# Expert weights and the first batch's denominators brought to their rows by transfers through HBM

## The chip, the cores and the metric

The kernel runs on one core of a Trainium2 chip. The metric is the device time of one execution in microseconds. A core has five engines that run at the same time: TensorE (PE, matrix products), VectorE (DVE), ScalarE (ACT), GpSimd (POOL) and SyncE (SP). In this kernel nearly all transfers between HBM and the on-chip memory (SBUF) are issued by SP, in the order of its own queue. Products of PE land in eight banks of a second memory, PSUM.

## What is computed

The reference is one transformer layer on `x` of 2 x 1024 tokens with 512 features, in float32. The layer adds two branches to its input, both computed from the normalised `xn`:

```
Q, K, V = heads(xn @ w.T + b)            # 16 heads of 32 features
Q, K = elu(Q) + 1, elu(K) + 1
out_attn = (Q @ (K^T V)) / (Q . sum(K) + 1e-8)  ->  @ wo.T + bo
scores = sigmoid(xn @ W_router)          # 8 experts
w = the two best of scores + bias, normalised; 0 elsewhere
gate = xn @ W_gate + shared low-rank + sum_e w_e * (xn @ A_e @ B_e)
up   = the same with its own matrices
out_ffn = (silu(gate) * up) @ W_down + low-rank terms
x + out_attn + out_ffn
```

Two values of this matter here. The **expert weights** `w` have one number for each token and expert; the kernel multiplies them into the low-rank factors `xn @ A_e`, which have 8 rows for each expert (rank 8), for gate and up. The **denominators** have one number for each token and head, and each divides the 32 features of its head.

## The kernel before

The 2048 tokens are two batches of 1024 (`NBATCH`), each in two groups `g` of 512 tokens (`TB`). Features lie on the 128 partitions in four chunks `c` of 128 (`NC`). The large products use seven block products in place of eight, so sums and differences of blocks are made on DVE and POOL. The order of the work on PE, DVE, ACT and POOL is the order of the program's text (`manual_schedule`, L67); SP's queue is ordered by the scheduler, by when data and buffers are ready.

The stages around the change, at 120 to 250 us of the profile:

- `query_unit(0)` (L957) makes the queries of batch 0. It calls hooks at named points (P2, P1, P6, P5, P7, P3, P4), after the products of the same number; a hook runs other work that is written into the order there. `route(n)` (L562) ranks the experts of group n and gives `ws[n]`, the tokens' expert weights, with tokens on the partitions.
- After it (L968 to L988): `shared_factors`; `load_weights(0)`, which loads the first gate and up weights; `spread_weights` (L590), which repeats each weight 8 times and for gate and up on POOL; `weights_across` (L600), which turns the spread weights by 4 transposes per group on PE and copies them by ACT to `wT[b]`, where rows are (gate or up, expert, rank) and columns are tokens; `low_rank_in` (L846), products with the factors `A`, times `wT` on DVE (L852), giving `xa`; `denominators(0)` (L856), 8 products and a reciprocal (L866), giving `den`, in which row `c * 32 + 8 * h + 4 * g` belongs to chunk c, head h of the chunk and group g; the last token sums of batch 1; `token_diffs` (L980) on POOL.
- `rest_weights` (L1006) loads and prepares the last 96 columns of gate and up.
- `query_unit(1)` (L1080) makes the queries of batch 1. Its hooks run `attend(0, g)` (L869): four products of a 0/1 matrix `spread` with `den` bring each denominator to the 32 rows of its head in PSUM, DVE multiplies the query tile by it (L878) and SP stores the tile (L881). `fold_rest(i)` (L1023) adds the shared low-rank term to the rest weights: 4 small products, 8 DVE additions (L1032).
- Then `low_rank_in(2)` and `(3)`, `denominators(1)`, `rest(0, ...)` (L1034), in which `fold(0, 0)` adds the low-rank term to the first gate weights (L938), and `attend(1, ...)`.

Tiles are taken from pools: a tile with a tag waits until the last use of the tile that had the buffer before. The pool for PSUM gives out eight banks.

Of the kernel before, what the change touches and what calls it, by code (L numbers as in the profile page):

```python
# [15 lines left out]
P = 128  # L16
# [21 lines left out]
def layer_kernel(  # L38
# [53 lines left out]
    NQ = UT // P  # L92
    NPQ = NC // 2
    WARM = 18

    TILES = [b * TPBATCH + g * TPB + t for b in range(NBATCH) for t in range(TPB) for g in range(2)]

# [16 lines left out]
    h_dram = [[dram.tile([2, P, 4, UT], F32, name=f"h_dram{b}_{j}") for j in range(NP)] for b in range(NBATCH)]  # L114
    r_dram = [dram.tile([2, REST, 2, UT], F32, name=f"r_dram{b}") for b in range(NBATCH)]
    q_dram = [[dram.tile([2, P, 4, UT], F32, name=f"q_dram{b}_{j}") for j in range(NPQ)] for b in range(NBATCH)]
    kvo_dram = [dram.tile([P, NC, D], F32, name=f"kvo_dram{b}") for b in range(NBATCH)]

    ffn_stack = ExitStack()
# [22 lines left out]
    def hold(v):  # L142

        nc.vector.memset(v, 0.0)
# [142 lines left out]
    def norm(n):  # L287

        k = n % 6
        xns[n] = (  # L290
            p1w.tile([P, D], F32, tag=f"xn{k}", name=f"xn{n}", bufs=1)
            if k < 4 else p2w.tile([P, D], F32, tag=f"qt{k - 2}1", name=f"xn{n}", bufs=1)
        )
# [261 lines left out]
    def shared_factors(i):  # L555
# [3 lines left out]
        )  # L559
        nc.scalar.mul(sat[:, i, :], pa[:, 0:P], SCALE)  # L560

    def route(n):  # L562

        sc = p2.tile([P, TPB, E], F32, tag="sc", name=f"sc{n}")
        nc.scalar.activation(sc, lg[n], AF.Sigmoid)
        bi = p2.tile([P, TPB, E], F32, tag="bi", name=f"bi{n}")
        nc.vector.tensor_add(bi, sc, eb_sb.unsqueeze(1).to_broadcast([P, TPB, E]))

        sh = [P, TPB, E, E]
        bj = bi.unsqueeze(2).to_broadcast(sh)  # L570
        be = bi.unsqueeze(3).to_broadcast(sh)
        gt = p2.tile(sh, F32, tag="gt", name=f"gt{n}")
        nc.vector.tensor_tensor(gt, bj, be, ALU.is_gt)
        eq = p2.tile(sh, F32, tag="eq", name=f"eq{n}")
        nc.vector.tensor_tensor(eq, bj, be, ALU.is_equal)
        nc.vector.tensor_mul(eq, eq, before.unsqueeze(1).to_broadcast(sh))
        nc.vector.tensor_add(gt, gt, eq)
        rank = p2.tile([P, TPB, E], F32, tag="rank", name=f"rank{n}")
        nc.vector.tensor_reduce(rank, gt, AX.X, ALU.add)
        ws = p2.tile([P, TPB, E], F32, name=f"ws{n}")  # L580
        nc.vector.scalar_tensor_tensor(ws, rank, TOP_K - 0.5, sc, ALU.is_lt, ALU.mult)
        sm = p2.tile([P, TPB], F32, tag="sm", name=f"sm{n}")
# [5 lines left out]
        return ws  # L588

    def spread_weights(n):  # L590

        wx = p2.tile([P, TPB, 2, ER], F32, tag="wx", name=f"wx{n}", bufs=2)
        for t in range(TPB):
            nc.gpsimd.tensor_copy(
                wx[:, t, :, :].rearrange("p i (e r) -> p i e r", r=RANK),
                ws[n][:, t, :].unsqueeze(1).unsqueeze(3).to_broadcast([P, 2, E, RANK]),
            )
        return wx

    def weights_across(n, wx):  # L600
        pw = bank(f"pw{n}")
        for t in range(TPB):
            nc.tensor.transpose(pw[:, ts(t, P)], wx[:, t, :, :].rearrange("p i r -> p (i r)"), ident)
        nc.scalar.copy(wT[n // 2][:, ts(n % 2, TB)], pw)

    tsum = []
    tsum_pair = []
# [69 lines left out]
    ws = {}  # L677

    def routed(n):
        ws[n] = route(n)  # L680

    hooks = {
        (1, "b"): [lambda: load_weights(wq_sb, wqT)],
# [11 lines left out]
        (7, "a"): [lambda: routed(0), lambda: fin[0].outputs((1,))],  # L695
        (7, "b"): [lambda: fin[0].outputs((2, 3))],
    }

    def load_weights(t, w):
        hold(t[:, 0, 0:1])  # L700
        nc.sync.dma_start(out=t, in_=by_chunk(w))
# [149 lines left out]
            nc.tensor.matmul(pa, agu_sb[:, c, :], xt(b, c, cols), start=(c == 0), stop=(c == NC - 1))  # L851
        nc.vector.tensor_mul(xa[b][:, cols], pa, wT[b][:, cols])  # L852

    dens = {}

    def denominators(b):  # L856

        pd = bank(f"pd{b}")
        for g in range(2):
            for c in range(NC):  # L860
                nc.tensor.matmul(
                    pd[c * 32 : (c + 1) * 32, :], ksd[b][:, g, c, :], qt[b, c, g], start=(g == 0), stop=(g == 1)
                )
        den = ffn.tile([P, TB], F32, tag="den", name=f"den{b}")
        nc.vector.tensor_scalar_add(den, pd, DIV_EPS)
        nc.vector.reciprocal(den, den)  # L866
        dens[b] = den

    def attend(b, g):  # L869

        pb = []
        for c in range(NC):
            rows = slice(c * 32, (c + 1) * 32)
            pb.append(bank(f"pb{b}_{g}_{c}"))
            nc.tensor.matmul(pb[c], spread[rows, g, :], dens[b][rows, :], start=True, stop=True)
        for c in range(NC):
            v = qt[b, c, g]
            nc.vector.tensor_mul(v, v, pb[c])  # L878

            j, i = c % NPQ, c // NPQ  # L880
            nc.sync.dma_start(  # L881
                out=q_dram[b][j][:, :, 2 * i + g, :].rearrange("s p n -> p s n"),
                in_=v.rearrange("p (s n) -> p s n", n=UT),
            )
# [5 lines left out]

    wsum = {}

    def load_weights(j):

        ws = []
        for i, w in enumerate((w_gate, w_up)):
            if j % 2 and i == 0:
                t = slot(8, [8, 2 * P], f"w{i}_{j}")
            elif j % 2:
                t = tsp.tile([P, 8, 2 * P], F32, tag="t3", name=f"w{i}_{j}")  # L900
            else:
                t = tsp.tile([P, 8, 2 * P], F32, tag=f"t{i}", name=f"w{i}_{j}")
            v = t.rearrange("p s (k m) -> p s k m", m=P)
            for half in range(2):
                f = (j + half * NP) * P
                nc.sync.dma_start(
                    out=v[:, 6 * half : 6 * half + 2, :, :].rearrange("p s k m -> p (s k) m"),
                    in_=by_chunk(w)[:, :, f : f + P],
                )
            ws.append(t)  # L910

        sb = ffn.tile([P, 2, 2, P], F32, tag="sb", name=f"sb{j}", bufs=2)
        for i, w in enumerate((b_gate, b_up)):
            for k in range(SG):
                nc.sync.dma_start(
                    out=sb[k * 32 : k * 32 + RANK, i, :, :],
                    in_=w[ER:LR, 0 : 2 * NP * P].rearrange("r (h n) -> r h n", h=2)[:, :, ts(j, P)],
                )
        wsum[j] = (ws, sb)
# [28 lines left out]
    def last_sums():  # L948
        add_keys(late)
        for args in late:  # L950
            accumulate(*args)
        for n in (1, 2):
            routed(n)
        fin.append(Finish(1, pg, ksum))
        fin[1].copies()

    query_unit(0, {  # L957
        "P2": [last_sums],
        "P6": [lambda: fin[1].chunk_sums(), lambda: fin[1].sums(), lambda: routed(3)],
        "P5": [lambda: fin[1].values()],  # L960
        "P7": [lambda: next(sums1), lambda: next(sums1)],
        "P3": [lambda: fin[1].outputs((0, 1, 2, 3))],
    })
    psum1.close()
# [4 lines left out]
        shared_factors(i)  # L969
    p1_stack.close()  # L970
    tsp = pool(ctx, "tsp", side="right")
    load_weights(0)
    wx = [spread_weights(n) for n in range(2)]
    for n in range(2):
        weights_across(n, wx[n])
    low_rank_in(0)
    low_rank_in(1)
    xdiff = []

    def token_diffs(b, tag):  # L980
# [53 lines left out]
    def rest(b, between=(None, None)):  # L1034
# [1063 lines left out]
```

## Time and profile before

| | us |
|---|---|
| median of 3 runs | 731.14 |
| lowest, highest | 730.44, 731.93 |
| profiled execution | 732.03 |
| its span | 730.2 |
| PE busy in the span | 719.9 (99%) |
| DVE busy | 579.99 |
| ACT, POOL busy | 199.80, 147.25 |
| PE clock granted | 0.996 |

The span is what the profile covers of the execution; 1.8 us lie around it. A row of a timeline gives start, duration, engine, line, operation, output and input tiles, shapes and a count; in brackets stands the idle time before it and what ended it. A float32 product of PE is two records. In the chain of work each piece is followed back to what released it. `SPq` rows are transfers being issued, not their data. Buffer numbers are left out of names: `pw` is `pw0` to `pw3`.

### The profile page before, as it was taken

How to read it: one execution, taken by the hardware profiler on the slowest of the kernel's cores; microseconds unless marked ns; L12 is line 12 of the kernel's file. 1: busy time of each engine (PE TensorE's matmuls, PEld its weight loads, DVE VectorE, ACT ScalarE, POOL GpSimd, SP SyncE). 2: the span in 40 equal slices, each digit the busy share in tenths (PEclk: the TensorE clock that was granted, in tenths of full speed). 3: DMA queues.
4: the chain of work that ended last, by engine and by line, in shares of the span. 5: the costliest groups of instructions: out<-in, count | busy, mean ns of one | idle time of the engine just before them, and what ended most of it. 6: DMA issues, size and time to landing. Idle time of an engine off the chain costs nothing.

```text
span 730.2 us, 9892 instructions
## 1 busy us (share of the span) xinstructions
PE 719.9 (99%) x3458; PEld 494.6 (68%) x3458; DVE 580.0 (79%) x1326; ACT 199.8 (27%) x440; POOL 147.3 (20%) x192
## 2 busy tenths in 40 slices
PE   8999999999999999999999999999999999999997
PEld 6666676454433556666666666666688899899896
DVE  6788766776777688878878878968888889998874
ACT  3534513454433323323333333333200000000000
POOL 4023011112000680410410410543520100000000
PEclk9999999999999999999999999999999999999999
DMA  5343000207314101211201201334653444523101
GB/s 168 98 130 116 1 0 37 61 1 188 120 29 126 37 5 57 88 33 58 87 29 58 87 29 59 111 121 144 202 180 117 125 146 134 166 95 110 58 17 43
DMA packets 59398, 63.37 MB, mean 87 GB/s; under 512 B 10066, under 2 KB 48594, under 8 KB 59092
## 3 DMA queue, kind: packets, MB, share of 16 engines
q1 hardware_dynamic: 58818, 62.72, 28.0%
q8 instruction: 27, 0.44, 0.3%
q14 instruction: 23, 0.19, 0.1%
q10 hardware_dynamic: 530, 0.02, 0.0%
HBM read 40.97 MB, written 21.76 MB: 86 GB/s over the span
## 4 chain that ended last, share of the span: by engine, by line
PE 84%; DVE 12%; ACT 1%; issue 1%; DMA 0%; DVEq 0%; ACTq 0%
PE ab L1179 16%; PE b L1239 8%; PE po L1875 7%; PE pg L398 5%; PE pqu L772 4%; PE pya L1747 4%; PE pxa L1747 3%; PE pyb L1747 3%; PE ph L1615 3%; PE x L1179 3%; PE pxb L1747 2%; PE pyc L1747 2%; PE b L1234 2%; PE pqv L772 2%; PE pxa L851 2%; PE pr L1073 2%
## 5 line engine op out<-in xcount | busy, mean ns | idle before, releaser
L1239 PE MATMUL b<-t,w 128*128 128x512 f32 x160 | 83.2, 601 | 0.8 <-DVE t L1261 0.8
L398 PE MATMUL pg<-kt,xn 128*128 128x512 f32 x128 | 58.7, 594 | 0.5 <-DVE kt L342 0.5
L1261 POOL TENSOR_TENSOR r<-r,r 128x512 f32<-128x512 f32 x20 | 30.1, 1524 | 84.6 <-DVE t L1261 83.0
L1179 PE MATMUL ab<-ti,wi 128*128 128x256 f32 x180 | 45.4, 379 | 0.0
L1179 PEld LDWEIGHTS ab<-ti,w 128*128 128x128 f32 x140 | 25.2, 189 | 29.5 <-DVE r L1207 8.3
L1261 DVE TENSOR_TENSOR r<-r,r 128x512 f32<-128x512 f32 x60 | 45.0, 791 | 0.0
L1179 PEld LDWEIGHTS ab<-ti,wi 128*128 128x128 f32 x180 | 34.2, 190 | 13.2 <-issue 5.0
L1179 PE MATMUL ab<-ti,w 128*128 128x256 f32 x140 | 41.2, 387 | 0.5 <-DVE r L1207 0.2
L398 PEld LDWEIGHTS pg<-kt,xn 128*128 128x128 f32 x128 | 23.1, 190 | 22.6 <-issue 20.6
L1212 ACT COPY r<-ab 128x256 f32<-128x256 f32 x50 | 18.6, 373 | 71.5 <-PE ab L1179 71.5
L1239 PEld LDWEIGHTS b<-t,w 128*128 128x128 f32 x160 | 29.2, 190 | 11.3 <-issue 5.9
L1207 DVE TENSOR_TENSOR r<-r,ab 128x256 f32<-128x256 f32 x50 | 21.0, 419 | 19.8 <-ACT r L1204 19.2
L1215 DVE TENSOR_TENSOR r<-r,ab 128x256 f32<-128x256 f32 x50 | 20.9, 418 | 16.2 <-ACT r L1212 15.8
L1189 ACT COPY r<-ab 128x256 f32<-128x256 f32 x50 | 18.6, 373 | 48.5 <-PE ab L1179 47.0
L1875 PE MATMUL po<-wd,f 128*128 128x256 f32 x140 | 30.9, 380 | 0.1
L407 POOL TENSOR_TENSOR ksum<-ksum,kt 128x512 f32<-128x512 f32 x12 | 15.8, 1320 | 71.7 <-DVE lg L444 42.3
L1200 ACT COPY r<-ab 128x256 f32<-128x256 f32 x50 | 18.6, 373 | 40.8 <-PE ab L1179 40.8
L1818 DVE TENSOR_TENSOR f<-f 128x256 f32<-128x256 f32 x84 | 29.4, 423 | 0.1
L1875 PEld LDWEIGHTS po<-wd,f 128*128 128x128 f32 x140 | 26.4, 190 | 4.4 <-issue 0.5
L1179 PE MATMUL ab<-xnT,w 128*128 128x256 f32 x100 | 29.4, 390 | 0.0
L1179 PE MATMUL ab<-xnT,wi 128*128 128x256 f32 x100 | 28.1, 379 | 0.0
L1179 PEld LDWEIGHTS ab<-xnT,w 128*128 128x128 f32 x100 | 18.1, 189 | 10.8 <-issue 4.3
(449 smaller groups left out, 1665.3 us busy)
## 6 DMA issues: line engine op xcount, KB each, us to landing
h_dram<-h SPq DMA_DIRECT2D x40, 256.0 KB
f<-h_dram SPq DMA_DIRECT2D x10, 512.0 KB
x_ring<-in_x_dram SPq DMA_DIRECT2D x16, 256.0 KB
q_dram<-qt SPq DMA_DIRECT2D x16, 256.0 KB
xr<-in_x_dram SPq DMA_DIRECT2D x16, 256.0 KB
out_dram<-xr SPq DMA_DIRECT2D x15, 256.0 KB
w<-in_w_gate_dram SPq DMA_DIRECT2D x10, 256.0 KB
w<-in_w_up_dram SPq DMA_DIRECT2D x10, 256.0 KB
```

Source lines behind the costliest of these rows:

```text
L398: nc.tensor.matmul(pg[m], xns[n][:, ts(m, P)], kt, start=(j == 0), stop=(j == TPBATCH - 1))
L772: nc.tensor.matmul(banks[c], wqs[p][:, k, ts(c, P)], tsum[b][p][:, k, :], start=(start and k == 0), stop=(k == 1), skip_group_check=True,)
L1179: nc.tensor.matmul(out, w, t, start=start, stop=True, skip_group_check=True)
L1189: nc.scalar.copy(self.r[0][:, H0], self.ua)
L1207: nc.vector.tensor_add(self.r[1][:, H1], self.r[1][:, H1], self.lo)
L1215: nc.vector.tensor_add(self.r[1][:, H0], self.r[1][:, H0], self.lo)
L1239: nc.tensor.matmul(pb[m], ws[m][:, A_OF[p], ts(k, P)], tsum[b][p][:, k, :], start=start, stop=True, skip_group_check=True)
L1261: eng.tensor_add(to[m], t[m], v[m])
L1615: nc.tensor.matmul(phs[u][g * ER : (g + 1) * ER, :], a, f[:, g, :], start=(ns[0] == 0 and n == 0), stop=(last and n == len(chunks) - 1), s ...
L1747: nc.tensor.matmul(o, lhsT, rhs, start=first, stop=True, skip_group_check=True)
L1818: op(t[:, at, :], t[:, x_, :], t[:, y, :])
L1875: nc.tensor.matmul(ps[p][:, q, :], lhsT, rhs, start=start, stop=stop, skip_group_check=True)
```

## The change

Expert weights: `route` writes the weights of both groups of a batch into one tile `wts[b]`. `weights_across(b)` transposes that tile once on PE (128 x 64), ACT copies it to `wx`, SP stores it to HBM (`w_dram`), and 16 transfers read it back, each copying one expert's 1024 weights to 8 rows of `wT[b]`. It is called in `query_unit(0)` at P5 (batch 0) and P7 (batch 1). `spread_weights` is gone.

Denominators of batch 0: `den` is stored to HBM (`d_dram`). `spread_den` reads four of its rows back, each to the 32 rows of a head, into one of three tiles `bc`; three such tiles are filled at once and the next after each multiplication. The multiplications come in four pairs, at P5, P7, P3 and P4 of `query_unit(1)`. Batch 1 keeps the products.

Around it: the low-rank products, `denominators(0)` and `token_diffs(0)` follow `rest_weights`, with `denominators(0)` between the two low-rank products; `load_weights(0)` moves to P4 of `query_unit(1)`, where small memsets on DVE hold its transfers back; `fold_rest(1)` moves from P4 to after `load_last`. Some tiles share buffers: `gt` takes a `tmp` buffer, `rank` that of `bi`, three `xn` tiles those of `bc`.

```
+    wts = [p2.tile([P, 2, TPB, E], F32, name=f"ws{b}") for b in range(NBATCH)]
...
-        gt = p2.tile(sh, F32, tag="gt", name=f"gt{n}")
+        gt = p2w.tile(sh, F32, tag="tmp", name=f"gt{n}", bufs=3)
...
-        rank = p2.tile([P, TPB, E], F32, tag="rank", name=f"rank{n}")
+        rank = bi
...
-        ws = p2.tile([P, TPB, E], F32, name=f"ws{n}")
+        ws = wts[n // 2][:, n % 2]
...
-    def spread_weights(n):
...
-    def weights_across(n, wx):
-        pw = bank(f"pw{n}")
-        for t in range(TPB):
-            nc.tensor.transpose(pw[:, ts(t, P)], wx[:, t, :, :].rearrange("p i r -> p (i r)"), ident)
-        nc.scalar.copy(wT[n // 2][:, ts(n % 2, TB)], pw)
+    def weights_across(b):
+        rows = 2 * TPB * E
+        pw = fin[1].bank(f"pw{b}")
+        nc.tensor.transpose(pw[0:rows, 0:P], wts[b].rearrange("p n t e -> p (n t e)"), ident)
+        wx = p2.tile([rows, P], F32, tag="wx", name=f"wx{b}")
+        nc.scalar.copy(wx, pw[0:rows, 0:P])
+        nc.sync.dma_start(out=w_dram[b].rearrange("e t p -> t e p"), in_=wx)
+        for i in range(2):
+            for e in range(E):
+                k = i * ER + e * RANK
+                nc.sync.dma_start(
+                    out=wT[b][k : k + RANK, :],
+                    in_=w_dram[b][e].rearrange("t p -> (t p)").partition_broadcast(RANK),
+                )
...
+    def spread_den():
+        i = len(bcs)
+        if i == 2 * NC:
+            return
+        g, c = divmod(i, NC)
+        t = p2w.tile([P, TB], F32, tag=f"bc{i % NBC}", name=f"bc{i}", bufs=1)
+        for h in range(HPC):
+            row = c * 32 + 8 * h + 4 * g
+            nc.sync.dma_start(out=t[h * DK : (h + 1) * DK, :], in_=d_dram[row, :].partition_broadcast(DK))
+        bcs[i] = t
...
         dens[b] = den
+        if b == 0:
+            nc.sync.dma_start(out=d_dram, in_=den)
+            for i in range(NBC):
+                spread_den()
...
-    def attend(b, g):
+    def attend(b, g=None):
+        if b:
...
+        else:
+            k = len(attended)
+            attended.extend((k, k + 1))
+            todo = [(i % NC, i // NC) for i in attended[-2:]]
+            by = [bcs[i] for i in attended[-2:]]
+        for (c, g), t in zip(todo, by):
             v = qt[b, c, g]
-            nc.vector.tensor_mul(v, v, pb[c])
+            nc.vector.tensor_mul(v, v, t)
+            if b == 0:
+                spread_den()
...
+                if late:
+                    hold(v[:, 6 * half : 6 * half + 2, 0, 0:1])
                 nc.sync.dma_start(
...
-        "P5": [lambda: fin[1].values()],
-        "P7": [lambda: next(sums1), lambda: next(sums1)],
+        "P5": [lambda: fin[1].values(), lambda: weights_across(0)],
+        "P7": [lambda: next(sums1), lambda: next(sums1), lambda: weights_across(1)],
...
-    load_weights(0)
-    wx = [spread_weights(n) for n in range(2)]
-    for n in range(2):
-        weights_across(n, wx[n])
-    low_rank_in(0)
-    low_rank_in(1)
...
-    denominators(0)
-    for _ in range(2):
-        next(sums1)
-    for n in range(2, 4):
-        weights_across(n, spread_weights(n))
-    token_diffs(0, "xd")
...
     w_rest = rest_weights()
+    low_rank_in(0)
+    denominators(0)
+    low_rank_in(1)
+    for _ in range(2):
+        next(sums1)
+    token_diffs(0, "xd")
     query_unit(1, {
-        "P1": [lambda: attend(0, 0)],
-        "P5": [lambda: attend(0, 1)],
-        "P7": [lambda: fold_rest(0)],
-        "P4": [lambda: fold_rest(1)],
+        "P5": [lambda: attend(0)],
+        "P7": [lambda: fold_rest(0), lambda: attend(0)],
+        "P3": [lambda: attend(0)],
+        "P4": [lambda: attend(0), lambda: load_weights(0, True)],
     })
...
     sb_d, wdr, bd_sb, wdr_diff, bd_diff = load_last()
+    fold_rest(1)
     low_rank_in(2)
```

More of the change, by code (lines that the diff above doesn't have):

```diff
@@ L94, in layer_kernel @@
     WARM = 18
+    NBC = 3
     TILES = [b * TPBATCH + g * TPB + t for b in range(NBATCH) for t in range(TPB) for g in range(2)]
@@ L116, in layer_kernel @@
     q_dram = [[dram.tile([2, P, 4, UT], F32, name=f"q_dram{b}_{j}") for j in range(NPQ)] for b in range(NBATCH)]
+    w_dram = [dram.tile([E, 2 * TPB, P], F32, name=f"w_dram{b}") for b in range(NBATCH)]
+    d_dram = dram.tile([P, TB], F32, name="d_dram")
     kvo_dram = [dram.tile([P, NC, D], F32, name=f"kvo_dram{b}") for b in range(NBATCH)]
@@ L291, in norm @@
             p1w.tile([P, D], F32, tag=f"xn{k}", name=f"xn{n}", bufs=1)
-            if k < 4 else p2w.tile([P, D], F32, tag=f"qt{k - 2}1", name=f"xn{n}", bufs=1)
+            if NBC <= k < 4 else p2w.tile([P, D], F32, tag=f"qt{k - 2}1" if k >= 4 else f"bc{k}", name=f"xn{n}", bufs=1)
         )
@@ L587, in route @@
         nc.vector.tensor_mul(ws, ws, sm.unsqueeze(2).to_broadcast([P, TPB, E]))
-        return ws
-    def spread_weights(n):
-        wx = p2.tile([P, TPB, 2, ER], F32, tag="wx", name=f"wx{n}", bufs=2)
-        for t in range(TPB):
[L594 to L598, printed above, removed]
-    def weights_across(n, wx):
-        pw = bank(f"pw{n}")
-        for t in range(TPB):
-            nc.tensor.transpose(pw[:, ts(t, P)], wx[:, t, :, :].rearrange("p i r -> p (i r)"), ident)
-        nc.scalar.copy(wT[n // 2][:, ts(n % 2, TB)], pw)
+    def weights_across(b):
[12 more added lines that the diff above has]
+                )
     tsum = []
@@ L676, in layer_kernel @@
     fin = []
-    ws = {}
-    def routed(n):
-        ws[n] = route(n)
     hooks = {
@@ L694, in layer_kernel @@
         (6, "b"): [lambda: fin[0].outputs((0,))],
-        (7, "a"): [lambda: routed(0), lambda: fin[0].outputs((1,))],
+        (7, "a"): [lambda: route(0), lambda: fin[0].outputs((1,))],
         (7, "b"): [lambda: fin[0].outputs((2, 3))],
@@ L852, in low_rank_in @@
         nc.vector.tensor_mul(xa[b][:, cols], pa, wT[b][:, cols])
-    dens = {}
+    dens, bcs = {}, {}
+    def spread_den():
[8 more added lines that the diff above has]
+        bcs[i] = t
     def denominators(b):
@@ L867, in denominators @@
         dens[b] = den
-    def attend(b, g):
[L871 to L876, printed above, removed]
+        if b == 0:
+            nc.sync.dma_start(out=d_dram, in_=den)
+            for i in range(NBC):
+                spread_den()
+    attended = []
+    def attend(b, g=None):
+        if b:
+            todo = [(c, g) for c in range(NC)]
+            by = []
+            for c in range(NC):
+                rows = slice(c * 32, (c + 1) * 32)
+                by.append(bank(f"pb{b}_{g}_{c}"))
+                nc.tensor.matmul(by[c], spread[rows, g, :], dens[b][rows, :], start=True, stop=True)
+        else:
[4 more added lines that the diff above has]
+        for (c, g), t in zip(todo, by):
             v = qt[b, c, g]
-            nc.vector.tensor_mul(v, v, pb[c])
+            nc.vector.tensor_mul(v, v, t)
+            if b == 0:
+                spread_den()
             j, i = c % NPQ, c // NPQ
@@ L891, in layer_kernel, with load_weights @@
     wsum = {}
-    def load_weights(j):
+    def load_weights(j, late=False):
         ws = []
@@ L952, in last_sums @@
         for n in (1, 2):
-            routed(n)
+            route(n)
         fin.append(Finish(1, pg, ksum))
@@ L958, in layer_kernel @@
         "P2": [last_sums],
-        "P6": [lambda: fin[1].chunk_sums(), lambda: fin[1].sums(), lambda: routed(3)],
-        "P5": [lambda: fin[1].values()],
-        "P7": [lambda: next(sums1), lambda: next(sums1)],
+        "P6": [lambda: fin[1].chunk_sums(), lambda: fin[1].sums(), lambda: route(3)],
+        "P5": [lambda: fin[1].values(), lambda: weights_across(0)],
+        "P7": [lambda: next(sums1), lambda: next(sums1), lambda: weights_across(1)],
         "P3": [lambda: fin[1].outputs((0, 1, 2, 3))],
```

## The prediction

> **What bounds the kernel now.** I read the page's busy shares first, then the chain of work around the edited lines, then what DVE and SP do beside it. TensorE is busy almost throughout:
>
> ```profile
> PE 719.9 (99%) x3458; PEld 494.6 (68%) x3458; DVE 580.0 (79%) x1326; ACT 199.8 (27%) x440; POOL 147.3 (20%) x192
> ```
>
> A busy share alone does not make a bound, so the chain of waits between 100 and 260 us matters more (start, us, engine, tile, line, records):
>
> ```profile
> 166.23 1.27 PE psa L557 x10
> 167.50 0.87 PE pw L603 x8
> 168.37 6.87 PE pxa L851 x16
> 175.24 1.85 PE pd L861 x16
> 177.09 1.02 PE pw L603 x8
> 178.11 3.44 PE pqx L772 x8
> 181.55 3.43 PE pqu L772 x8
> 184.98 1.07 PE pb L875 x8
> 186.05 7.07 PE pqu L772 x16
> 193.12 1.07 PE pb L875 x8
> 194.19 3.63 PE pqv L772 x8
> ...
> 212.76 1.85 PE pd L861 x16
> ```
>
> Every piece is PE and each starts where the last ended; from 100 to 260 us nothing but PE appears. What leaves PE here shortens the run, until another engine becomes late. Whether one does is read from DVE (timeline), the next PE work that needs it, and SP's issues (tile view: ns min/median/max; then chain):
>
> ```profile
> 199.32 1.00 DVE L1032 TENSOR_TENSOR w_rest<-w_rest,pfr 128x64 f32<-128x64 f32 x8
> ...
> 206.97 0.88 DVE L781 TENSOR_SCALAR eq<-qt,bq_sb 128x512 f32<-128x512 f32 x2
> ...
> 209.90 0.69 DVE L784 TENSOR_TENSOR qt<-qt,eq 128x512 f32<-128x512 f32 x1 [0.44 <-ACT eq L783]
> ...
> 215.46 3.60 PE L1063 MATMUL pr<-xnT,w_rest 128*64 128x512 f32 x16
> ```
> ```profile
> L1020 SPq DMA_DIRECT2D w_rest<-in_b_up_dram x4: 288/295/337, 176.6 to 177.7; - x4
> L881 SPq DMA_DIRECT2D q_dram<-qt x16: 359/360/677, 187.0 to 234.8; - x16
> ...
> 0.74 2.90 DMA x_ring<-in_x_dram
> ```
>
> A small transfer costs SP 0.3 us, and a 256 KB one landed 2.5 us after its 0.4 us issue.
>
> **PE, the sum.** Removed: both `pw` groups, 0.87 + 1.02; both `pb` groups of batch 0, 1.07 + 1.07; and what each `pb` costs its successor: 8 records of L772 take 3.43 us elsewhere, 3.63 after `pb` (7.07 against 6.87 for 16), so 0.20 twice. That is 4.43 us. Added: two transposes at 0.87/8 = 0.11 each, and 0.20 for the second `pxa`, which now follows the 32-column `pd` (in the trace the piece after `pd` is 0.15 longer: 1.02 against 0.87). Net **-4.0 us**. The order is now `psa`, `pxa0`, `pd`, `pxa1`, `pqx`. `pd` at 171.2 needs the last query tile of L784; it is ready at 170.7.
>
> **Weights' path.** ACT takes two small copies for four of 0.6 us and has idle time there. The copy to `wx` gates one later PSUM bank: ready at about 161.4, wanted by the fourth `pko` at 162.1. SP: store `w_dram0` at 152.8, landing by 155.7; then 16 loads of 8 rows. At 0.3 us each they end at 160.5 and land at 163. DVE's L852 wants them at 171.2; `den`, its reciprocal and the token sums queue behind it. So 8 us of cover; without it DVE would delay `pqv`, which needs `t34`.
> A rule of the Trainium skill (page "DMA: Bandwidth & Descriptors", section Rules for kernel authors) speaks against this: an outermost dimension of c < 16, such as a broadcast of c copies, keeps a DMA on c engines. Here c is 8. The trace has 340 GB/s for large loads at 170 to 175 us, so by the rule 512 KB runs at half of that, 3.1 us, less than the 4.8 us that issuing 16 takes. By row or rule the sum is the same while issue sets the pace. The page also gives each transfer a fixed 2 us, mostly completion (section Anatomy of one DMA). Paid in series by 16 loads that is 32 us: DVE 16 us late, `t34` at 196.7 in place of 180.2, `pqv` 6 us late, and the change loses 2. But four L1020 issues followed each other at 0.3 us, so they overlap. I take the row.
>
> **Denominators' path, SP.** The built queue orders: `kvo_dram1` (167.0), 16 loads of `wT1`, 12 of `w_rest`, `d_dram`, two `w_1`, `wdr`, then 12 `bc` loads. The eighth `wT1` reuses the completion semaphore of `kvo_dram1`, which in this trace landed 4.8 us after issue: 172. Nine more at 0.3: 174.7. `w_rest` 4.0 us (2 x 0.43, 2 x 0.39, 8 x 0.3): 178.7, still far ahead of its user `pfr` (194). `den` is ready at 177.1, so `d_dram` waits 1.6 us for SP, lands at 181.6; eight `bc` loads 184.0, landed 186.5. The first `attend` comes up on DVE at 193.3 - 2.8 = 190.5: 4 us of cover.
> No row shows a broadcast read from HBM. Below: no cheaper than 0.3 us a piece. Above: 0.5 us for all 40 issues makes the first pair 4 us late, of which DVE's idle time before L819 takes 1.5. I take 0.3, the nearest row.
>
> **Denominators' path, DVE.** The eight multiplies stay (0.68 from PSUM; 0.69 for L784 with SBUF operands), but sit later, in pairs of 1.3. On before's clock: L1032 ends at 200.3, pair two 201.6, two L784 202.9, two L781 204.3, pair three 205.6, two L784 206.9, two L831 208.2, then 3.6 for L781 to the last L784 (as 206.97 to 210.6): 211.8. Less 4.0: **207.8**. `pd` starts at 208.8 and wants those tiles in its third and fourth product: 1.0 us of slack or more. Pair four 209.1, four memsets of 0.06, L1032 x8 at 210.3; L1063 wants it at 211.5: slack 1.2. DVE idles 1.7 us before L938, which takes up the remainder.
> The ring of three makes `bc5` tightest: released by the third multiply at 197.0, four issues, 2.5 landing: 200.7, wanted at 201.0. `bc3` has 6.0 us and `bc7` 7.4 where 3.7 are needed. So a reload may take 5.1 us, 3.9 there plus 1.2 slack, before PE loses anything. Behind a waiting multiply stand L784, L781 and L831, for which ACT and then `pd` wait; behind a `bc` load that waits on SP for its buffer stand the `q_dram` stores, the next `bc`, `w_1` and `w_0`.
>
> **The rest.** POOL loses sixteen `wx` copies (nothing on the chain); `xdiff0` moves behind the `w_rest` memset and copies, 1.1 us, and is first read after 260. The token sums of batch 1 follow the reciprocal as before. `gt` in the rotating buffer and `rank` over `bi` stay within DVE's order: nothing. `w_0` (four of 256 KB) moves from 167 to after the memsets, 209.4: behind two `q_dram` stores and one `w_1` load, 1.75 MB at 340 GB/s land by 217, wanted by L938 at 224.2 - 4.0 = 220.2. Cover 3 us; each us beyond goes first into L938, then `pb`. Its factors `sb` still load at the start. `fold_rest(1)` keeps its place on PE, after the same `pqv`.
>
> **Sum.** The profiled execution took 732.03 (span 730.2 and 1.8 around it); less 4.0, 728.0. It was 0.9 above the median of 731.14, so against the runs: **727.1**.
>
> **Rivals.**
> 1. *Part given back* (728 to 730, say 729): reloads of `bc` of 5.5 to 6.5 us, or issues of 0.4 to 0.5, leave DVE late by 1 to 3 us at `pd` or L1063. For it: SP's lane waits, one L1020 issue took 1.28 us. Against: SP issued nothing between 132 and 167.
> 2. *Slower*: the reload of `bc` at DVE's multiply (L878). Thirty-two copies of one HBM row may drain far slower than 340 GB/s. With reload time R, the pairs lose (R - 6.0) + (R - 3.9) + (R - 7.4), each from zero up, less 1.2. At R = 7.5 that is 4.0 and the gain is gone; beyond it each us costs 3, so R = 9 gives 735.6. Against: a tile is only 256 KB, 0.75 us at the trace's rate.
> 3. *Nothing comes of it* (731): DVE, 81% busy at 194 to 206 us, becomes the bound and keeps its old end. For it: it has 1 us to spare by my sum. Against: it lags PE there only through ACT's answers, which move with PE.
> 4. *More*: 726, if the 0.8 us weight-load waits around `pb` were time too.
>
> **How the numbers follow.** Full gain 0.68 (own range 726.0 to 728.3, from rival 4 and 0.2 us per switch), part 0.17, nothing 0.08, slower 0.07. Three runs of before spread over 0.2%, 1.5 us, which is what a measurement tells from no change. Faster by more: 0.68 + 0.16 of the second; within: 0.08 + 0.01; slower 0.07. The range leaves out rivals 2 and 3 and the worst of 1: 725.6 to 730.4.
>
> **What would show it.** Right: no `pw` L603 group, two single transposes near 152 and 156, no `pb` before 220, `pqu` in 6.87, and the chain still all PE with `pd` of batch 1 near 208.8; DVE's multiplies follow their predecessors without a DMA as releaser. Wrong: DVE waiting on `bc` or `wT` for over 1 us, `pd` or L1063 starting after a DVE release, or L938 waiting on `w_0`. A slow SP (issues over 0.5 us) or reloads over 5 us would make the forecast wrong.

## The result, and the profile after

The changed kernel takes 729.31 us (median of 12 runs, 728.21 to 730.40), the kernel before, run beside it, 732.63 (12 runs, 730.44 to 733.80). The ratio of the means is 0.9958, with a 95% interval of 0.9944 to 0.9972: faster by 3.1 us, between 2.1 and 4.1. The forecast was a gain of 4.0 and, from the median of 731.14 of the first three runs, 727.1.

The page of the changed kernel, first its busy shares:

```profile
PE 717.8 (99%) x3428; PEld 493.1 (68%) x3428; DVE 579.8 (80%) x1330; ACT 198.1 (27%) x438; POOL 143.4 (20%) x176
```

PE has lost 2.1 us of its 719.9, POOL the copies. The chain of work around the edits (start, us, engine, tile, line, records):

```profile
154.04 0.11 PE pw L598
154.15 3.44 PE pqv L772 x8
157.59 0.12 PE pw L598
...
166.35 1.94 ACT gt L554 x4
168.30 0.04 issue
168.34 1.38 PE psa L560 x10
169.72 3.44 PE pxa L851 x8
173.16 1.85 PE pd L873 x16
175.01 3.63 PE pxa L851 x8
178.65 3.43 PE pqx L772 x8
182.08 10.30 PE pqu L772 x24
192.38 3.43 PE pqv L772 x8
...
210.75 1.85 PE pd L873 x16
```

Two single transposes stand for the `pw` groups, no `pb` appears before the second `pd`, 24 records of `pqu` run without a break, and the second `pxa` costs 3.63. One thing is new: between 157.7 and 168.3 the chain is no longer PE. It goes through the queries' DVE and ACT work to ACT's four copies of `pko` (their output is `gt`), and these release `psa`. PE's own timeline has the wait in brackets:

```profile
168.34 1.38 PE L560 MATMUL psa<-ident,sa 128*128 128x128 f32 x10 [0.35 <-ACT gt L554]
```

On DVE one row in the stretch waits for a transfer, 0.57 us at the second multiply of the third pair (`bc5`); the last query tile (L784) and the rest weights (L1049) are ready before `pd` at 210.75 and before `pr` at 213.62, and the fold sums of `w_0` (L967) wait for PE, not for their load:

```profile
203.21 0.69 DVE L903 TENSOR_TENSOR qt<-qt,bc 128x512 f32<-128x512 f32 x1 [0.57 <-DMA bc<-d_dram]
...
209.14 0.69 DVE L784 TENSOR_TENSOR qt<-qt,eq 128x512 f32<-128x512 f32 x1 [0.44 <-ACT eq L783]
...
211.12 0.86 DVE L1049 TENSOR_TENSOR w_rest<-w_rest,pfr 128x32 f32<-128x32 f32 x7
...
222.20 1.41 DVE L967 TENSOR_TENSOR w<-w,pf 128x256 f32<-128x256 f32 x4 [1.26 <-PE pf L958]
```

SP's issues, by tile (ns, min/median/max):

```profile
L605 SPq DMA_DIRECT2D wT<-w_dram x32: 263/293/1196, 156.5 to 175.9; - x32
L865 SPq DMA_DIRECT2D bc<-d_dram x32: 303/419/1308, 183.4 to 205.9; - x32
```

With the gap to the next issue, one of `wT` takes 0.37 us of SP's time (16 in 5.95) and one of `bc` 0.45 (4 in 1.81), where the sum had 0.3. The reload of `bc5` is the exception. Its four issues, the first row here, took 2.58 us, the last of them 1.31 alone; the four of `bc6`, the second row, took the usual time:

```profile
198.94 2.58 SPq L865 DMA_DIRECT2D bc<-d_dram  x4
...
202.10 1.80 SPq L865 DMA_DIRECT2D bc<-d_dram  x4
```

**A measure that the start leaves alone.** The two profiled executions took 732.03 and 730.10, only 1.9 apart. Part of the gain is hidden by the start. The chain in the first 10 us, of the changed kernel and then of the one before:

```profile
6.51 1.08 PE pt L308 x4
7.59 2.00 PE pbk L676 x2
```
```profile
6.54 0.67 PE pt L305 x4
7.21 1.05 PE pbk L672 x2
```

The same first products took 1.36 us longer in the profile after, and `pv`, the last piece ahead of the edits, ends at 154.04 there and at 152.49 in the one before. So all runs below are also compared by one stretch of their profiles: from the end of `pv` to the first `ab` product (`ab` L1179, after the change L1202). It took 152.49 to 245.15, **92.66 us**, and now takes 154.04 to 243.14, **89.10**: a gain of **3.56**. From `ab` to the end of the span both have 485.1 (485.05 and 485.16), so nothing is given back later. The stretch repeats well: kernels that differ only outside it or in the place of `w_0` agree within 0.02 us (92.66 twice; 89.10, 89.11 and 89.12).

### The profile page after: what moved, and what is told of

It reads as the page before. It is cut to its first block, busy times and chain, and to the rows that moved or that the text cites. A ratio compares the mean times of both kernels' runs of the same rounds, so it can differ in the third digit from the quotient of the medians.

```text
span 728.3 us, 9908 instructions
## 1 busy us (share of the span) xinstructions
PE 717.8 (99%) x3428; PEld 493.1 (68%) x3428; DVE 579.8 (80%) x1330; ACT 198.1 (27%) x438; POOL 143.4 (20%) x176
## 4 chain that ended last, share of the span: by engine, by line
PE 83%; DVE 12%; ACT 3%; issue 1%; DMA 0%; DVEq 0%; ACTq 0%
PE ab L1202 16%; PE b L1262 8%; PE po L1899 7%; PE pg L401 5%; PE pya L1771 4%; PE pxa L1771 3%; PE pqu L772 3%; PE pyb L1771 3%; PE ph L1639 3%; PE x L1202 3%; PE pxb L1771 2%; PE pyc L1771 2%; PE pxa L851 2%; PE b L1257 2%; PE pr L1090 2%; PE pye L1771 2%
## 5 line engine op out<-in xcount | busy, mean ns | idle before, releaser
L1202 PE MATMUL ab<-ti,wi 128*128 128x256 f32 x180 | 45.4, 379 | 0.0
L1202 PEld LDWEIGHTS ab<-ti,w 128*128 128x128 f32 x140 | 25.1, 189 | 29.4 <-DVE r L1230 8.2
L1202 PEld LDWEIGHTS ab<-ti,wi 128*128 128x128 f32 x180 | 34.2, 190 | 13.2 <-issue 5.0
L1202 PE MATMUL ab<-ti,w 128*128 128x256 f32 x140 | 41.2, 387 | 0.5 <-DVE r L1230 0.2
L401 PEld LDWEIGHTS pg<-kt,xn 128*128 128x128 f32 x128 | 23.2, 190 | 22.6 <-issue 20.6
L1202 PE MATMUL ab<-xnT,w 128*128 128x256 f32 x100 | 29.4, 390 | 0.0
L1202 PE MATMUL ab<-xnT,wi 128*128 128x256 f32 x100 | 28.1, 379 | 0.0
L1202 PEld LDWEIGHTS ab<-xnT,w 128*128 128x128 f32 x100 | 18.1, 189 | 10.8 <-issue 4.5
```

What stands on the lines that cost most here:

```text
L401: nc.tensor.matmul(pg[m], xns[n][:, ts(m, P)], kt, start=(j == 0), stop=(j == TPBATCH - 1))
L1202: nc.tensor.matmul(out, w, t, start=start, stop=True, skip_group_check=True)
```

## The experiments

| run | stretch, us | median of runs, us | ratio to before (95%) |
|---|---|---|---|
| before | 92.66 | 732.63 beside the changed kernel | |
| changed | 89.10 | 729.31 | 0.9958 (0.9944 to 0.9972) |
| weights alone | 91.65 | 730.91 | 0.9977 (0.9967 to 0.9986) |
| denominators alone | 90.13 | 729.37 | 0.9967 (0.9954 to 0.9979) |
| changed, other bank | 88.64 | 728.88 | 0.9950 (0.9936 to 0.9965) |
| changed, `w_0` early | 89.11 | 727.89 | 0.9942 (0.9923 to 0.9962) |
| before, longer warm-up | 92.66 | 730.69 | 0.9976 (0.9968 to 0.9984) |
| changed, longer warm-up | 89.12 | 727.79 | 0.9942 (0.9928 to 0.9956) |
| reload in 8 loads | 92.85 | 732.10 | 1.0004 (0.9991 to 1.0018) |
| reload in 16 loads | 101.93 | 741.32 | 1.0129 (1.0109 to 1.0149) |
| one load for a tile | 90.59 | 730.18 | 0.9975 (0.9964 to 0.9987) |
| one load, bank, warm-up | 90.37 | 728.31 | 0.9946 (0.9928 to 0.9963) |
| the same, both batches | - | 739.18 | 1.0101 (1.0082 to 1.0120) |
| bank and warm-up | 88.66 | 727.33 | 0.9928 (0.9914 to 0.9941) |

The stretch has one value for each kernel, from its profile; medians of few runs move by about 1 us with the start that they happened to have. The run without a value has its first `ab` ahead of the delay, so the stretch would not show it.

### Do PE's pieces add?

**The weights alone.** The denominators keep their products:

```
-        if b == 0:
-            nc.sync.dma_start(out=d_dram, in_=den)
-            for i in range(NBC):
-                spread_den()
...
-        if b:
+        if True:
             todo = [(c, g) for c in range(NC)]
...
-        "P5": [lambda: attend(0)],
-        "P7": [lambda: fold_rest(0), lambda: attend(0)],
-        "P3": [lambda: attend(0)],
-        "P4": [lambda: attend(0), lambda: load_weights(0, True)],
+        "P1": [lambda: attend(0, 0)],
+        "P5": [lambda: attend(0, 1)],
+        "P7": [lambda: fold_rest(0)],
+        "P4": [lambda: load_weights(0, True)],
```

> The weights go through HBM as in the changed kernel, the denominators of batch 0 are spread by the four pairs of products as before. Measure: from the end of pv (before the edits) to the first ab product, 92.66 us in the kernel before and 89.10 in the changed one. Theory (PE's pieces add up): the two pw groups leave (-0.87 and -1.02), two transposes come (+0.22), the second pxa after pd costs +0.20, and psa waits for the fourth copy of pko (+0.33): 91.5 us, 1.1 faster than before. Rival (DVE keeps its own end, PE's pieces don't add): close to the whole gain of 3.5 or none.

Measured: 150.94 to 242.59, 91.65 us, a gain of 1.01. `psa` starts 14.32 us after `pv`'s end, as in the changed kernel (14.30) and later than before (13.74).

**The denominators alone.** The old spread on POOL and the four transposes a group are back (the spread weights in the buffer that `w_0` uses later, since SBUF has no room beside it):

```
-        "P5": [lambda: fin[1].values(), lambda: weights_across(0)],
+        "P5": [lambda: fin[1].values()],
...
+    wxs = tsp.tile([P, 8, 2 * P], F32, tag="t0", name="wxs")
+    wx = [spread_weights(n) for n in range(2)]
+    for n in range(2):
+        weights_across(n, wx[n])
...
-    denominators(0)
     low_rank_in(1)
+    denominators(0)
...
+    for n in range(2, 4):
+        weights_across(n, spread_weights(n))
```

> The denominators of batch 0 go through HBM as in the changed kernel, the weights are spread by GpSimd copies and transposed as before. Theory: the two pb groups leave (-1.07 twice) and so does the 0.20 that each costs its successor: the stretch from pv's end to the first ab takes 92.66 - 2.54 = 90.1 us, 2.5 faster than before; psa doesn't wait, since pko has its old banks. Rival (reloads of the denominators give a part back): under 2.0 faster, with DVE waits on transfers of over 1 us. The two parts alone should add to the whole change (1.1 + 2.5 against 3.56).

Measured: 152.54 to 242.67, 90.13 us, a gain of 2.53. Its chain, where the two `pb` groups were:

```profile
181.60 10.30 PE pqu L772 x24
191.90 3.43 PE pqv L772 x8
```

The parts add: 1.01 and 2.53 are 3.54, the whole is 3.56. DVE does not keep an end of its own.

**Another bank for `pw`.** In the changed kernel the two `pw` transposes are drawn from the four banks that `pko`'s tiles rotate through. That moves `pko` on by two: before, `psa`'s first bank was the one of the second `pko` tile, now it is that of the fourth, which ACT copies last. One line puts both `pw` in the fourth bank and starts `pko` at the first:

```
+        fin[1].made = NC - 1
         pw = fin[1].bank(f"pw{b}")
```

> The changed kernel, with both pw transposes in the fourth bank of the pool, so that pko's four tiles take banks 0 to 3 and psa's first bank is free after the first pko copy. Theory (the hand-over of the bank cost 0.33 us at psa): psa starts as soon as pqv ends, and the stretch from pv's end to the first ab takes 88.8 us, 0.3 less than the changed kernel's 89.10. Rival (the gap is ACT's copies being late whatever the bank, or DVE gives it back later): 89.1.

The chain of this run has PE alone again, and no gap between `pqv` and `psa`:

```profile
162.95 3.43 PE pqv L773 x8
166.38 1.27 PE psa L560 x10
```

Measured: 152.43 to 241.07, 88.64 us, 0.46 less than the changed kernel. The 0.46 is the wait of 0.35 and 0.11 that `psa` itself takes longer after it (1.38 against 1.27). With it the gain over the kernel before is 4.02. ACT itself is not later: its fourth copy ends 14.2 us after `pv` in the kernel before (166.7) and in the changed one (168.3).

**`w_0` at its old place.**

```
     tsp = pool(ctx, "tsp", side="right")
+    load_weights(0)
...
-        "P4": [lambda: attend(0), lambda: load_weights(0, True)],
+        "P4": [lambda: attend(0)],
```

> The changed kernel, with the four loads of w_0 back at their old place ahead of the weights' loads. Theory (the move costs nothing and hides nothing): the stretch from pv's end to the first ab takes 89.1 us as in the changed kernel, within 0.1. Rival (at the old place they hold SP's queue or the DMA engines, and the weights or the denominators come late): over 89.5, with DVE waiting on wT or bc.

Measured: 152.37 to 241.48, 89.11 us. The move costs nothing and brings nothing. (Four runs; the median of 727.89 is below the changed kernel's because two of them, 727.19 and 727.24, lie in a lower cluster; neither was profiled.)

### The start

The 27 to 35 runs of the kernel before that stood beside most groups of runs fall in three clusters: near 730.3, 731.9 and 733.6. The profiles of all kernels with 18 warm-up transposes show why: `pv` ends at 150.6 to 150.9, at 152.2 to 152.5 or at 154.0 to 154.1, though the first 100 us are the same work. What the start costs stays to the end: `pv` ends at 154.04, 152.37 and 151.13 in the changed kernel, in that with `w_0` early and in that with the longer warm-up below, and the spans are 728.3, 726.7 and 725.5. The rows of the window 6.4 to 12 us (us of the window, then busy us of PE, PEld, DVE, ACT, POOL with counts, granted clock, DMA share, GB/s) of the weights alone (`pv` at 150.94), of the kernel before (152.49) and of the changed one (154.04):

```profile
6.40:12.00 5.60, 5.59 (x26) 3.95 (x26) 4.02 (x13) 1.54 (x6) 4.13 (x4) 1.00 0.62 187
```
```profile
6.40:12.00 5.60, 5.46 (x16) 3.78 (x17) 4.03 (x13) 1.33 (x4) 3.91 (x4) 0.70 0.63 195
```
```profile
6.40:12.00 5.60, 5.49 (x12) 3.21 (x13) 2.73 (x10) 1.43 (x4) 4.17 (x4) 1.00 0.62 183
```

PE is busy in all three, but gets 26, 16 or 12 records done. In the second the granted clock says so: 0.70 in this window, 0.50 between 8.5 and 11.5 us. There the first products are fast, and the twelve records of `pk` behind them take 4.55 us in place of 2.90. In the third the granted clock stands at 1.00, and only the duration of a product tells: 1.00 us for each `pbk` against 0.53. To test whether more warm-up changes this, its transposes were raised from 18 to 24 in both kernels, to bring their end nearer to the first `pt`:

```
-    WARM = 18
+    WARM = 24
```

> The kernel before, with 24 warm-up transposes at the start in place of 18, so that PE is busy up to the first pt at about 6.4 us. Theory (the runs of one kernel differ by when PE leaves its slow start: the two pbk products took 1.05 us in the profile of before and 2.00 in that of the changed kernel): the slowest group of runs, 733.3 to 733.9, goes, and the rest stays at 730.3 to 732. Rival (the groups come from elsewhere, or the longer warm-up only shifts the work): the same spread of 3.5 us, or all 1 us later.

Measured: 22 runs, 730.05 to 731.51, none in the clusters at 731.9 and 733.6; the median of 730.69 is 1.4 below that of the kernel before beside it (732.05). So more warm-up removes the slow clusters. Why is not shown: PE still stands idle for 0.57 us before `pt` in this profile and for 0.87 in the next, and 18 transposes end at 5.47 us both in the fast start (the weights alone) and in the slow one (the changed kernel).

> The changed kernel, with 24 warm-up transposes in place of 18. Theory: the group of runs at 730.0 to 730.4 goes, leaving 728.2 to 728.6 or a group below; against the kernel before with the same warm-up the difference of medians is then the change itself, 3.4 to 3.6 us. Rival (the difference of the two kernels is in part the start, moved by the other buffers of xn): under 3 us.

Measured: six runs, 727.25 to 727.99, median 727.79. The slow clusters are gone in this kernel too. The difference of the two medians is 2.90, not 3.4 to 3.6, and by the words on record that is the rival's. Yet the stretches of their profiles differ by 3.54 (92.66 and 89.12) and their spans by 3.4 (728.9 and 725.5), and the 22 runs of one still spread over 1.5 us. Six runs do not settle 0.6 us; whether some of the start's effect is left in the medians stays open.

### How far the reloads may be late

**Eight loads a reload.** From the fourth `bc` tile on:

```
+            n = DK // 2 if i >= NBC else DK
+            for r in range(h * DK, (h + 1) * DK, n):
-            nc.sync.dma_start(out=t[h * DK : (h + 1) * DK, :], in_=d_dram[row, :].partition_broadcast(DK))
+                nc.sync.dma_start(out=t[r : r + n, :], in_=d_dram[row, :].partition_broadcast(n))
```

> The changed kernel, with each reload of bc (the fourth tile on) cut into 8 loads of 16 rows in place of 4 of 32: same bytes, twice the issues, 1.8 us more for each at the 0.45 us that an issue took. Theory of the prediction (a reload may take 5.1 us; it took 4.3): now about 6.1, so DVE waits some 2.2 us at bc5, 1.2 of it is absorbed, and the stretch from pv's end to the first ab is 90.2 us, up to 91.1 if SP's own queue of loads adds up. Rival (there is more cover than the sum had): 89.1.

DVE's rows that waited for a transfer, and SP's rows around the fifth and sixth tile:

```profile
201.77 0.69 DVE L905 TENSOR_TENSOR qt<-qt,bc 128x512 f32<-128x512 f32 x1 [1.51 <-DMA bc<-d_dram]
205.93 0.69 DVE L905 TENSOR_TENSOR qt<-qt,bc 128x512 f32<-128x512 f32 x1 [3.46 <-DMA bc<-d_dram]
214.34 0.69 DVE L905 TENSOR_TENSOR qt<-qt,bc 128x512 f32<-128x512 f32 x1 [1.18 <-DMA bc<-d_dram]
```
```profile
195.52 4.66 SPq L867 DMA_DIRECT2D bc<-d_dram  x8
200.22 0.42 SPq L910 DMA_DIRECT2D q_dram<-qt  x1
200.74 3.64 SPq L867 DMA_DIRECT2D bc<-d_dram  x8
```

Measured: 152.25 to 245.10, 92.85 us, 3.75 over the changed kernel: the whole gain is gone, and the loss is more than either figure expected. `bc5`'s buffer was free at 197.1, but SP was still issuing `bc4`'s eight loads, then a store; `bc5`'s began at 200.7 and had landed by 205.9, 8.8 us after the release. A reload's time is not only its own issues and landing; it is also what stands in SP's queue ahead of it (`bc4`'s eight took 4.66 us, one of them 1.42). Before `pd`, DVE waited 1.51 + 3.46 = 4.97 us, and PE lost 3.75 of it: 1.2 us of cover.

**Sixteen loads a reload** (`DK // 4` in the same lines).

> The changed kernel, with each reload of bc cut into 16 loads of 8 rows: 7.2 us of SP issues for a tile. By the prediction's formula for its slower case, with a reload of 9.7 us: 3.7 + 5.8 + 2.3 - 1.2, 10.6 us over the changed kernel; with SP's queue as the limit (five tiles of 7.2 us after 193 us, the last landing at 231 where it is wanted at 210) up to 20. Either way slower than before: the stretch takes 100 to 109 us. Rival (DVE's order hides it): under 93.

Measured: 150.59 to 252.52, 101.93 us, 12.8 over the changed kernel, inside the span expected, though `bc5` took 13.7 us from its buffer's release and not 9.7. DVE waited for `bc` 1.29, 3.33, 5.12 and 5.42 us.

**One load for a tile.** If SP's issues are the limit, fewer should help: one load for each `bc` tile, and one for each half of `wT`:

```
-        for h in range(HPC):
-            row = c * 32 + 8 * h + 4 * g
-            nc.sync.dma_start(out=t[h * DK : (h + 1) * DK, :], in_=d_dram[row, :].partition_broadcast(DK))
+        rows = d_dram[c * 32 : (c + 1) * 32, :].rearrange("(h x) n -> h x n", x=8)[:, 4 * g, :]
+        nc.sync.dma_start(out=t, in_=rows.unsqueeze(1).to_broadcast([HPC, DK, TB]))
...
-            for e in range(E):
...
+            src = w_dram[b].rearrange("e t p -> e (t p)").unsqueeze(1).to_broadcast([E, RANK, 2 * TPB * P])
+            nc.sync.dma_start(out=wT[b][i * ER : (i + 1) * ER, :], in_=src)
```

> The changed kernel, with each bc tile filled by one load (four rows of d_dram, each to 32 partitions) in place of four, and each half of wT by one load in place of eight. Same bytes, SP issues of these go from 64 to 12. Theory (what delays a reload is SP's issue time, and in the changed kernel the delay is covered): the 0.57 us DVE wait at bc5 goes, the stretch from pv's end to the first ab stays at 89.1. Rival (a rule of the Trainium skill, page DMA: Bandwidth & Descriptors, section Rules for kernel authors: an outermost dimension of 4 or 8 keeps a transfer on so many engines): a 256 KB reload at a quarter of 340 GB/s takes 3.1 us beside the 2, no faster than four issues, DVE waits 0.5 to 1 us more, and the stretch takes 89.1 to 90.

Its chain leaves PE at the reload. The two rows behind it are of windows in which nothing but one `bc` load, and nothing but `wT` loads, were under way (columns as in the windows above):

```profile
199.03 6.53 DMA bc<-d_dram
```
```profile
199.60:200.20 0.60, 0.60 (x3) 0.19 (x2) 0.60 (x3) 0.00 (x0) 0.00 (x0) 1.00 0.26 99
158.00:161.00 3.00, 3.00 (x8) 1.33 (x7) 2.97 (x5) 2.06 (x3) 0.00 (x0) 1.00 0.50 135
```

Measured: 154.11 to 244.70, 90.59 us, 1.49 worse than the changed kernel, and beyond the rival's 90. One load of four rows, each to 32 partitions, keeps the 16 DMA engines 0.26 busy, four of them; one of eight rows, each to eight, 0.50. That is what the Trainium skill states (page "DMA: Bandwidth & Descriptors", section Rules for kernel authors): an outermost dimension of c < 16 confines a transfer to at most c engines. The reload takes 6.5 us from its issue. At 99 GB/s its 256 KB are 2.6 us (an estimate); other loads and stores run in that time, and how much each of them adds stays open. DVE waits 2.86 at `bc5` in place of 0.57; PE loses 1.49 of it, and 1.4 is cover. In the changed kernel each load has 32 copies outermost. Between 187 and 189 us, with nothing but `bc` loads under way, the row is

```profile
187.00:189.00 2.00, 2.00 (x6) 0.95 (x5) 0.65 (x2) 0.60 (x2) 0.00 (x0) 1.00 0.56 153
```

153 GB/s is one load of 64 KB in 0.43 us, about the time of an issue, so there the issues set the pace and not the engines. Four issues a tile cost SP 1.8 us, and their rate is still half as high again as that of the single load.

### Versions meant to be faster

**The bank, the warm-up and the single loads together** (the edits above).

> The changed kernel with both pw in the fourth bank (0.46 us in the run with that alone), 24 warm-up transposes and one load for each bc tile and each half of wT. If the parts add: the stretch from pv's end to the first ab 88.6 us, the median 0.45 below the 727.8 of the changed kernel with the longer warm-up: 727.3. Rival (the single loads are slower): 727.8 or more.

Measured: 728.31 us, stretch 151.33 to 241.70, 90.37: the rival's. DVE waits 3.10 at `bc5`. The single loads cost 1.7 us against the run with the bank alone (88.64), more than the 0.46 that the bank gains.

**The same for both batches**: `denominators(1)` stores to a second HBM tensor, and `attend(1, g)` multiplies by loaded tiles in six buffers.

```
-        if b == 0:
-            nc.sync.dma_start(out=d_dram, in_=den)
-            for i in range(NBC):
-                spread_den()
+        nc.sync.dma_start(out=d_dram[b], in_=den)
+        for i in range(NBC * (b + 1)):
+            spread_den(b)
...
-                nc.tensor.matmul(by[c], spread[rows, g, :], dens[b][rows, :], start=True, stop=True)
+            by = [bcs[b][g * NC + c] for c in range(NC)]
```

> The last kernel, and the denominators of batch 1 through HBM too, with six buffers (bc and the three of tmp), so that the group of pb products at 226.67 (2.41 us) goes as well. If DVE and the stores stay ahead: the stretch 86.2 us, the median 2.4 lower, 724.9. Rival (r_dram's stores, the loads of w and the reloads share SP's queue at 217 to 235 us, and DVE comes late at the fold sums or wi): a part of the 2.4 or a loss, with a DVE wait on bc.

Measured: 739.18 us, 7.3 slower than the kernel before beside it (731.88). The `pb` products are gone from PE, but the chain now leaves PE for the reloads and for a store of a query tile behind them:

```profile
222.91 14.32 DMA bc<-d_dram
...
237.75 7.71 DMA q_dram<-qt
```

Seven of the eight multiplies wait for a transfer, 1.2 to 2.6 us each. The tiles follow each other at 1.9 to 3.3 us, and the gated rows behind them on DVE wait too; PE then stands idle for 7.9 us. The likely reason is that each load has four engines. Four loads a tile were not tried here, so it stays open whether batch 1 could gain.

**The bank and the warm-up, loads as in the change.**

> The changed kernel with its loads as they are, both pw in the fourth bank and 24 warm-up transposes. If the two parts add (0.46 us measured for the bank alone, in the stretch): pv's end to the first ab 88.6 us, the median 0.45 below the 727.79 of the longer warm-up alone, 727.3, with no run above 728. Rival (the bank's gain is given back by DVE, which then waits longer at bc5): 727.8.

Measured: 727.33 us (five runs, 726.43 to 727.63), ratio 0.9928 (0.9914 to 0.9941), whose interval lies below that of the changed kernel, 0.9944 to 0.9972. The bank's share of this, 0.46, is read from the stretch (151.93 to 240.59, 88.66 against 89.12); the medians, five and six runs with overlapping intervals, do not tell this version from the longer warm-up alone. DVE now waits longer at `bc5`, where one of the four issues took 2.12 us, and PE loses nothing by it:

```profile
201.47 0.69 DVE L904 TENSOR_TENSOR qt<-qt,bc 128x512 f32<-128x512 f32 x1 [1.40 <-DMA bc<-d_dram]
```

This version is faster than both kernels.

## Why the prediction was right, and where it was off

**PE's sum.** Right. Without the wait at `psa` the stretch shrinks by 4.02 us, where the sum had 4.0. The denominators' part, 1.07 twice and 0.20 twice, was 2.54; alone it measured 2.53. So the weight-load waits around `pb` were no time of their own, and rival 4 falls. Two of the signs named for "right" were not met: the chain leaves PE ahead of `psa`, and one multiply waits for a transfer (0.57 us).

**The weights' path: the step that failed.** The sum had -0.87, -1.02, +0.22 and +0.20, 1.47 less; alone it measured 1.01. The step read "the copy to `wx` gates one later PSUM bank" and followed that bank to the fourth `pko`, which indeed did not wait. It did not follow the rotation on: two more tiles from four banks also move every later tile, and the one after `pko` is `psa`, in a new pool on the same banks. Its bank went from ACT's second copy of `pko` to its fourth. That is the 0.46 between 4.02 and 3.56, shown by the run with the other bank. The rest of the path held: no wait on `wT`, the fourth `pko` not late, though an issue took 0.37 us and not 0.3. The fixed 2 us that the prediction took from the page is stated there for transfers issued by GpSimd, and here SP issues; the store of `wx` (issued at 154.47, first load of `wT` at 156.51) took about as long. It was not paid in series: 16 loads were issued in 5.95 us.

**The denominators' path.** Right in its order and in which place is tightest, off in sizes. `bc5` was named as tightest, ready 0.3 us before it was wanted; it came 0.57 late, about 4.3 us from release to use and not 3.7. The usual four issues, 1.81 us and not 1.2, would not have made it late; its own took 2.58, and less the 0.77 between them it would have come 0.2 ahead (an estimate). In the six profiles with four loads a tile, one issue of `bc5` took 1.28 to 2.12 us and DVE's wait went with it, from 0.54 to 1.40. In the same half microsecond each of these traces has one transfer of about 16 KB on the queue of kind `instruction`; beside the reloads around it in the changed kernel and in the last run there is none. That the issue waits for it is likely, and no run tests it. The cover ahead of `pd`, 1.0 to 1.2 us in the sum, is 1.2 to 1.4 by the eight-load, single-load and last runs, so the 0.57 was absorbed. The first pair had its tiles in time.

**Rival 2, the slower case.** It did not come in the changed kernel. The runs with more loads brought it on, and its formula asks too much: at the 8.8 us of `bc5` in the eight-load run it gives 7.9 us (2.8 + 4.9 + 1.4 - 1.2), at the 13.7 of the sixteen-load run 22.6, and 3.75 and 12.8 were measured. It adds the delays of the pairs, but they overlap: DVE's wait of 1.51 us for `bc4` lies inside the time that `bc5`'s reload has anyway. For the eight-load run the one term of `bc5` is enough: 8.8 - 3.9 - 1.2 is 3.7. The mechanism was put in the wrong place, too. Thirty-two copies of one row did not drain slowly; SP's queue of issues was near full, and doubling the number of reload issues was enough to undo the change. The single loads showed the other edge, engines left idle. My own sum was weak here: it let each reload begin at the release of its buffer, with SP free.

**Rival 1, part given back**, named issues of 0.4 to 0.5 us, and they came (0.45, and one of 1.31), but DVE was not late at `pd` for it; the part that was lost went at a place it did not name. **Rival 3** falls with the parts that add. **`w_0`** and the other moves at nothing: right, by the run with `w_0` early and by L967, which waits for PE.

**The total.** 727.1 was low by 2.2 us: 0.5 is the bank, 1.5 that the kernel before has a median of 732.63 over 12 runs and not 731.14, and the rest, some 0.3, is within what the sampling of the start moves. So the number alone would have misled: 729.31 lies outside the 726.0 to 728.3 that the prediction gave its full gain, and inside the 728 to 730 of rival 1, whose mechanism did not occur. The prediction took the spread of three runs, 1.5 us, as noise; over 12 runs it is 3.4 us, it is the start, in clusters, and it is as large as the gain.

## What to carry to other kernels

When a change draws extra tiles from a small rotating set of banks, follow the rotation to the first tile after the loop, not only to the next user of that bank. Work moved from PE to transfers has its limit in the issuing queue: count the issues of all tiles between two users, not the time of one tile, and before merging issues look at what the outermost dimension of the merged transfer would be. Compare small changes by a stretch of the trace that begins after the start, since here the start alone differed by as much as the gain.

## What the runs showed of the hardware

- PE's start is not the same in each execution: the first two 512-column products took 1.05 to 2.00 us, and by the end of `pv` the profiles lie in three groups up to 3.5 us apart. The granted clock shows one of the slower starts (0.70 at 6.4 to 12 us) and not the other (1.00). In the one that it shows, it is 0.83, 0.50, 0.50, 0.50 and 0.97 in the five microseconds from 7.5, which makes 3.4 us at half speed (an estimate). The Trainium skill (page "TensorE: Matmul & The Clock Gate", Part 1) says that PE runs at half speed until a window of some 3.4 us has been busy, and that the window does not begin with the kernel. The doubled products and the 3.4 us agree with the first; no run here shows when the windows begin.
- A broadcast load of 64 KB costs SP 0.45 us of issue time, one of 32 KB 0.37, when they follow each other. Single issues took up to 2.12 us.
- A 256 KB load with four rows outermost kept 0.26 of the DMA engines busy, at 99 GB/s; the same bytes in four loads of 32 copies each reached 0.56 and 153 GB/s, at the pace of their issues. One load with eight rows outermost kept 0.50 busy.
